# Adaptive-norm attention with a routed feed-forward: where the mask, the late weights and the keys' product stand in the attention stage

## The chip, the cores and the metric

One core of one Trainium2 chip runs the whole kernel. The metric is the time of one execution on the device in microseconds (us); of several executions the median is taken, and lower is better.

A core has a matrix engine (TensorE, PE in the profile; PEld is its weight load), a vector engine (VectorE, DVE), a scalar engine (ScalarE, ACT), GpSimd (POOL) and SyncE (SP), which here only asks for transfers. Each engine works through its own list of instructions in order, and semaphores make one engine wait for another. Transfers (DMA) asked for by SP, POOL or ACT run beside the engines.

## The reference, cut to what matters

The input `x` is 16 sequences of 512 tokens with 512 features. First comes attention with one shared head of keys and values and 16 heads of queries, 64 wide:

```python
xn  = layernorm(x) * g_in
q   = (xn @ Wq) * DH**-0.5          # 16 heads
k,v = split(xn @ Wkv)               # one head, shared; one null key and value in front
sim = q @ k.T + bias[head]          # bias: (16, 512, 512), the same for every sequence
sim = where(causal or token mask, -max, sim)
out = layernorm((softmax(sim) @ v) @ Wo) * g_out
```

Then a mixture of 16 experts follows: a root-mean-square norm, router logits, the top 512 tokens of each expert, two layers of 2048 hidden units, a weighted scatter back, and the sum with `x`.

All of the change lies in the attention. Two things matter there. The additive bias of a head is the same for all 16 sequences, and its causal part (-2^100 above the diagonal) is the same for all heads, so a bias that was once masked on the chip can be kept in device memory and read again.

## The kernel before

**Stages.** The attention stage takes the span from its start to about 1885 us; routing and the experts follow. The attention works on pairs: pair `p` is sequence `b = p // 8` and head pair `hp = p % 8`, which makes 128 pairs. `HP` is 8, `QB` (blocks of 128 queries) is 4, `DC` (chunks of 128 features) is 4, `B` is 16.

**Order.** Nearly every engine is wrapped in `Pinned` (line 119): its instructions are issued in the order in which the Python program makes them, and all of them carry line 129 in the profile. Only calls through `nc.` directly are placed by a scheduler. So the order of the loop body (`for p in range(B * HP + 1)`, from line 652) is the order on each engine. `Pair` objects overlap: while pair `p` has its scores reduced, the queries of pair `p + 1` are multiplied (`ahead`), the probabilities of pair `p - 1` are transposed and moved (`behind`), and the value product of pair `p - 2` is made (`turned.attend()`).

**The body of one pair, in order.** SP asks for the bias of pair `p + 1` (`load_bias`, tile `bias`, 1.31 MB, two buffers). PE makes the scores of blocks 3, 2 and 0 (`sp`); DVE adds the bias and takes the minimum of the negated row in one custom instruction (`reduce`: `p<-sp,bias,nn_sb`, with `nm`), ACT takes exponentials (`exps`). `late` norms get their root of mean square (`root`: a power on POOL, `rms_r`). DVE transposes the probabilities of pair `p - 1` in 32x32 squares (`behind.turn`: `sq<-p`), then 16 DMAs move the squares (`behind.move`: `pt<-sq`), ten asked for by SP and six by POOL. **Then, in the first eight pairs, POOL masks the bias of pair `p + 1`** (`mask_bias`: four affine selects of 128x256 numbers on the diagonal blocks) **and writes all of it to the device table `causal`**; from sequence 1 on `load_bias` reads `causal`. At `p == 1` POOL asks for the weights of later stages (`later_weights`, lines 195 to 200). Then come the scores and reduction of block 1, the statistics of the layer norms (`n.a()`: `ln_s`, `ln_mv`, `ln_t` on DVE and **the power on POOL**, `ln_r` or `lo_r`), the row sums, the value product `ap` with its copy `ot` on ACT, the application of the norms (`n.b()`: `xn` or `z` on DVE, for `z` also a multiplication on POOL), the division of the probabilities by their sums (`normalize`), and what `first` holds for this pair: transposes of the next sequence's normed input (`turn`: `xtp`, `xnt`), its keys and values (`keys_values`: `kp` on PE, `ka` on ACT, `vt` on DVE, and a small DMA `ka<-ka`), the transposed values (`turn_values`: `vtp`) and its token mask (`mask`: load `m8`, then `km` on DVE).

**PSUM.** `ps_s` (four buffers) holds scores, `ps_m` (three buffers) holds `qp`, `op`, `ap`, `xfp` and `kp`, `ps_t` (one buffer) holds `xtp` and `vtp`.

The order around the change in the loop body:

```python
if p + 1 < HP:
    mask_bias(p + 1, biases[p + 1])
if p == 1:
    later_weights()
...
for n in chains: n.a()
if now: now.sums()
if turned: turned.attend()
for n in chains: n.b()
...
for part in first.get(p, ()): part()     # keys_values among them
```

Of the kernel before, what the change touches and what calls it, by code (L numbers as in the profile page):

```python
# [8 lines left out]
F32 = mybir.dt.float32  # L9
# [3 lines left out]
U8 = mybir.dt.uint8  # L13
# [13 lines left out]
def tile_adaln_ffn(  # L27
# [111 lines left out]
    with ExitStack() as st:  # L139
# [54 lines left out]

        def later_weights():
            ge.dma_start(out=wo_sb, in_=wo.rearrange("(c p) n -> p c n", p=P))
            ge.dma_start(out=g_out_sb, in_=g_out.partition_broadcast(P))
            ge.dma_start(out=nw_sb, in_=norm_w.partition_broadcast(P))
            ge.dma_start(out=rw_sb, in_=router_w.rearrange("(c p) e -> p c e", p=P))
            ge.dma_start(out=rb_sb, in_=router_b.partition_broadcast(P))  # L200

# [41 lines left out]
        def load_bias(p):  # L243

            bt = biasp.tile([P, 2, SW], F32, name=f"bias_{p}", tag="bias")
            sy.dma_start(out=bt, in_=causal[p % HP] if p >= HP else bias[p])
            return bt

        def mask_bias(p, bt):


            with tc.issue_after(ge.last.ins):
                for q in range(QB):
                    diag = bt[:, :, off[q] + ext[q] - P : off[q] + ext[q]]
                    ge.affine_select(
                        out=diag, in_=diag, pattern=[[0, 2], [-1, P]],
                        compare_op=ALU.is_ge, fill=-BIG, base=0, channel_multiplier=1,
                    )
            ge.dma_start(out=causal[p], in_=bt)

        class Sequence:
# [13 lines left out]
            def turn(self, t):  # L275
# [11 lines left out]
                else:  # L287
                    ve.tensor_tensor(
                        dst, tp, g_in_sb.unsqueeze(2).to_broadcast([P, DC, P]), ALU.mult
                    )  # L290

            def mask(self):
                m8 = small.tile([DH + 1, N], U8, name=f"m8_{self.b}", tag="m8", bufs=1)
                self.km = kms[self.b % 2]
                for r in (0, DH):
                    nc.sync.dma_start(out=m8[r : r + 1, :], in_=mask[self.b : self.b + 1, :])
                for r in (0, DH):
                    ve.tensor_scalar(
                        self.km[r : r + 1, :], m8[r : r + 1, :], BIG, -BIG, ALU.mult, ALU.add
                    )  # L300

            def keys_values(self, i):

                if i == 0:
                    self.ka = seq.tile([P, N], F32, name=f"ka_{self.b}", tag="ka")
                    self.vt = seq.tile([DH, N], F32, name=f"vt_{self.b}", tag="vt")
                toks = slice(i * N // 2, (i + 1) * N // 2)  # L310
                kp = ps_m.tile([P, N // 2], F32, name=f"kp_{self.b}_{i}", tag="m")
                for c in range(DC):
                    te.matmul(
                        kp, wvk_sb[:, c, :], self.xnt[:, c, toks], start=(c == 0), stop=(c == DC - 1)
                    )
                se.activation(self.ka[DH:, toks], kp[DH:, :], AF.Identity, bias=vk_col[DH:, :])
                ve.tensor_scalar(self.vt[:, toks], kp[:DH, :], vk_col[:DH, :], None, ALU.add)
                nc.sync.dma_start(out=self.ka[:DH, toks], in_=self.ka[DH:, toks])

# [278 lines left out]

        halves, norms, routes, first, ins, loads = {}, {}, {}, {}, {}, {}
        early = HP - 3  # L600
        for b in range(B):
# [12 lines left out]
            if b + 1 <= end:  # L614
                ts, ks, v = ((0, 1, 2, 3), (2, 4), 5) if b else ((1, 2, 3, 4), (3, 5), 6)
                for t, k in enumerate(ts):
                    first.setdefault(at + k, []).append(lambda b=b, t=t: seqs[b + 1].turn(t))
                for i, k in enumerate(ks):
                    first.setdefault(at + k, []).append(lambda b=b, i=i: seqs[b + 1].keys_values(i))
                first.setdefault(at + v, []).append(lambda b=b: seqs[b + 1].turn_values())  # L620
                first.setdefault(at + 4, []).append(lambda b=b: seqs[b + 1].mask())
            if b + 2 <= end:
# [6 lines left out]
        seqs[0].xts = x0  # L629
        biases = {0: load_bias(0)}  # L630
        for pair in ((0, 1), (2, 3)):
            begun = [InNorm(seqs[0], t) for t in pair]
            for n in begun:
                n.a()
            for n in begun:
                n.b()
# [15 lines left out]
        for p in range(B * HP + 1):  # L652
            b, hp = divmod(p, HP)
            now, ahead = ahead, None
            if p + 1 < B * HP:
                biases[p + 1] = load_bias(p + 1)
                ahead = Pair(seqs[(p + 1) // HP], (p + 1) % HP)
# [18 lines left out]
            if now and behind:  # L676
                behind.turn()
                behind.move(sy, range(6, SN * SN))
                behind.move(ge, range(6))
            if p + 1 < HP:  # L680
                mask_bias(p + 1, biases[p + 1])
            if p == 1:
                later_weights()
            if 0 <= p - HP < NT // P:
# [20 lines left out]
            if now:  # L705
                now.sums()
            if turned:
                turned.attend()
            for n in chains:
                n.b()  # L710
            if now:
                now.normalize(0)
                now.normalize(3)
# [631 lines left out]
```

## Time and profile before

| what | value |
|---|---|
| median of 3 runs | 3617.39 us (3615.78 to 3621.26) |
| the profiled execution's own time | 3619.08 us |
| its span, from the first to the last instruction | 3617.40 us |
| PE busy | 3436.0 us (95%) |
| DVE busy | 2326.7 us (64%) |
| ACT busy | 1588.6 us (44%) |
| POOL busy | 904.7 us (25%) |
| `bias<-in_bias_dram` on SP, 1280 KB | 8 |
| `bias<-causal` on SP, 1280 KB | 120 |
| `causal<-bias` on POOL | 8, landing after 5.4 to 8.8 us |
| affine select on a bias, POOL | 32, median 402 ns |
| SP asks for squares (`pt<-sq`) | 1270 |
| mean granted clock of PE | 0.978 |

The profiled execution is 1.7 us above the median of the three runs, and 1.7 us longer than its span. A span counts from the first instruction to the last; busy time of one engine lies beside that of the others, and only what no other engine's work covers adds to the time. The granted clock is the share of its full clock that PE is given.

### The profile page before, as it was taken

The page shows a single profiled execution, that of the slowest core. Times are in us where ns is not written, and L with a number is a line of the kernel's source. Part 1 is how long each engine was busy: PE and PEld are TensorE (multiplying, and loading weights), DVE is VectorE, ACT ScalarE, POOL GpSimd, SP SyncE. Part 2 cuts the span into 40 slices and gives each one's busy share as a digit, 9 for nine tenths or more (in the row PEclk, how much of TensorE's full clock was granted, in tenths as well). Part 3 has the DMA queues.
Part 4 walks back from the last instruction along what each step waited for, and adds up shares of the span by engine and source line. Part 5 has one row for each costly group of instructions (what it writes and reads, how often), then busy time and mean ns, then how long its engine had stood idle before and what let it go on. Part 6 is the DMA issues. An engine that isn't in the chain of part 4 may idle for free.

```text
span 3617.4 us, 52129 instructions
## 1 busy us (share of the span) xinstructions
PE 3436.0 (95%) x16972; PEld 2477.8 (68%) x16972; DVE 2326.7 (64%) x6026; ACT 1588.6 (44%) x4160; POOL 904.7 (25%) x1332
## 2 busy tenths in 40 slices
PE   7899999999999999999993699999999999999999
PEld 3455555655556555655551588888888888888887
DVE  6676767667677777677547865555655566655553
ACT  5676667667676776667650211111112112111111
POOL 3333233333333333332320222211112112222110
PEclk9999999999999999999995899999999999999999
DMA  8877777677776666666542233333333334333330
GB/s 288 250 219 218 220 223 215 216 222 226 221 219 194 209 210 205 192 202 199 184 133 105 82 110 121 110 94 89 105 123 120 120 123 123 111 122 112 108 97 12
DMA packets 255045, 583.58 MB, mean 161 GB/s; under 512 B 48263, under 2 KB 117575, under 8 KB 236343
## 3 DMA queue, kind: packets, MB, share of 16 engines
q1 hardware_dynamic: 207360, 462.95, 38.6%
q0 software_dynamic: 45024, 114.44, 13.3%
q8 instruction: 136, 2.23, 0.3%
q10 hardware_dynamic: 2391, 2.85, 0.2%
q14 instruction: 134, 1.10, 0.1%
HBM read 366.41 MB, written 61.87 MB: 118 GB/s over the span
## 4 chain that ended last, share of the span: by engine, by line
PE 79%; DVE 8%; DMA 3%; SPq 3%; issue 2%; ACT 1%; POOL 1%; DVEq 0%; POOLq 0%; ACTq 0%
PE op L129 10%; PE r_y L129 9%; PE qp L129 9%; PE sp L129 7%; PE pa L129 6%; PE pc L129 6%; PE pc_y L129 6%; PE pa_y L129 6%; PE ap L129 6%; PE pd L129 3%; PE pe L129 3%; PE pb L129 3%; SPq L129 3%; DVE sq L129 2%; PE xfp L129 2%; DVE p L129 2%
## 5 line engine op out<-in xcount | busy, mean ns | idle before, releaser
L129 ACT ACTIVATE p<-p,nm 128x512 f32<-128x512 f32 (+3 forms) x1024 | 561.9, 550 | 256.4 <-DVE nm L129 254.9
L129 DVE CUSTOM_DVE_ANT_0 p<-sp,bias,nn_sb 128x512 f32<-128x512 f32 (+3 forms) x1024 | 499.8, 544 | 181.1 <-PE sp L129 165.4
L129 POOL DMA_DIRECT2D pt<-sq x762 | 381.3, 507 | 929.4 <-issue 561.7
L129 PE MATMUL qp<-xnt,wq_sb 128*128 128x512 f32 x1024 | 516.7, 628 | 0.0
L129 PE MATMUL op<-wo_sb,ot 128*128 128x256 f32 x1920 | 454.7, 382 | 1.1 <-ACT ot L129 1.1
L129 PEld LDWEIGHTS op<-wo_sb,ot 128*128 128x128 f32 x1920 | 358.8, 190 | 98.6 <-issue 53.9
L129 DVE STREAM_TRANSPOSE sq<-p 128x896 f32<-128x896 f32 x762 | 398.4, 587 | 25.0 <-ACT p L129 9.9
L129 ACT ACTIVATE p<-p,rs 128x512 f32<-128x512 f32 (+2 forms) x768 | 406.2, 603 | 1.8 <-DVE rs L129 1.1
L129 POOL DMA_INDIRECT out_dram<-y,tok x64 | 105.9, 1654 | 1181.0 <-ACT y L1174 1181.0
L1082 ACT ACTIVATE h<-h,b_sb 128x512 f32<-128x512 f32 (+1 forms) x256 | 143.5, 608 | 523.7 <-DVE h L129 523.7
L129 PE MATMUL sp<-ka,qa 64*128 64x512 f32 (+3 forms) x2048 | 358.6, 440 | 1.6 <-ACT qa L129 1.6
L1174 ACT ACTIVATE y<-y,gg 128x512 f32<-128x512 f32 x64 | 46.2, 722 | 646.9 <-DVE y L129 646.9
L129 PE MATMUL ap<-pt,vp 128*64 128x512 f32 (+3 forms) x2048 | 306.1, 440 | 2.7 <-ACT qa L129 1.1
L129 PEld LDWEIGHTS qp<-xnt,wq_sb 128*128 128x128 f32 x1024 | 176.2, 192 | 184.5 <-issue 169.1
L129 PEld LDWEIGHTS ap<-pt,vp 128*64 128x64 f32 x2048 | 146.3, 137 | 179.0 <-issue 142.2
L129 PE MATMUL pa<-xe,w 128*128 128x256 f32 x1024 | 243.4, 381 | 0.0
L129 PEld LDWEIGHTS sp<-ka,qa 64*128 64x128 f32 x2048 | 173.7, 189 | 89.9 <-issue 84.0
L129 PE MATMUL pa_y<-w,h 128*128 128x256 f32 x1024 | 231.5, 379 | 0.0
L129 PE MATMUL r_y<-w2t,hs 128*128 128x256 f32 x1024 | 231.5, 379 | 0.0
L129 PEld LDWEIGHTS pa<-xe,w 128*128 128x128 f32 x1024 | 195.6, 191 | 26.8
L129 PEld LDWEIGHTS r_y<-w2t,hs 128*128 128x128 f32 x1024 | 194.6, 190 | 26.4
L129 PEld LDWEIGHTS pa_y<-w,h 128*128 128x128 f32 x1024 | 193.4, 190 | 25.7
(201 smaller groups left out, 5193.9 us busy)
## 6 DMA issues: line engine op xcount, KB each, us to landing
bias<-causal SPq DMA_DIRECT2D x120, 1280.0 KB
w<-in_fc_dram SPq DMA_DIRECT2D x256, 512.0 KB
pt<-sq SPq DMA_DIRECT2D x1270, 80.0 KB
pt<-sq POOLq DMA_DIRECT2D x762, 80.0 KB, 3.1
x<-in_x_dram SPq DMA_DIRECT2D x64, 256.0 KB
out_dram<-in_x_dram SPq DMA_DIRECT2D x64, 256.0 KB
table<-xf SPq DMA_DIRECT2D x64, 256.0 KB
bias<-in_bias_dram SPq DMA_DIRECT2D x8, 1280.0 KB
```

Of the source, the lines that this page charges most:

```text
L129: self.last = tc.keep_in_program_order(made(*args, **kwargs))
L1082: nc.scalar.activation(a[0], a[1], AF.Gelu, bias=b1_sb[:, self.e, f : f + 1])
L1174: nc.scalar.activation(y, y, AF.Copy, scale=self.gg[:, g, self.e : self.e + 1])
```

## The change

Seven edits, all in the attention stage:

1. The later weights are asked for by SP and not by POOL, one transfer in each of the pairs 2 to 7, `wo` in two halves; they were asked for by POOL in pair 1, all five at once.
2. A bias is masked again in each of the first sequences until it is stored: `kept_in(hp)` is the sequence in which head pair `hp` is stored (0 for 6 and 7, 1 for 4 and 5, 2 for 2 and 3, 3 for 0 and 1). So there are 20 maskings (80 affine selects) and still 8 writes, two a sequence in sequences 0 to 3. Until its stored copy is read, a bias comes from `in_bias_dram`.
3. `mask_bias` moves from behind the squares' DMAs to behind `n.b()`, so the powers of the norms stand in front of it on POOL.
4. `keys_values` moves in front of `turned.attend()`, and `kp` is a tile of `ps_t` instead of `ps_m`.
5. The load of the token mask (`m8`) is split off, made on SP in program order, one pair ahead of its use.
6. The bias of pair 1 is asked for before the loop, behind the token mask of sequence 0.
7. The DMA of the keys (`ka<-ka`) is pinned to program order.

On PE only the eight `kp` matmuls change their place against `ap`. On DVE and ACT only `vt<-kp` and `ka<-kp` do.

```diff
-        def later_weights():
-            ge.dma_start(out=wo_sb, in_=wo.rearrange("(c p) n -> p c n", p=P))
-            ge.dma_start(out=g_out_sb, in_=g_out.partition_broadcast(P))
-            ge.dma_start(out=nw_sb, in_=norm_w.partition_broadcast(P))
-            ge.dma_start(out=rw_sb, in_=router_w.rearrange("(c p) e -> p c e", p=P))
-            ge.dma_start(out=rb_sb, in_=router_b.partition_broadcast(P))
+        later = [
+            (wo_sb[:, : HP // 2, :], wo.rearrange("(c p) n -> p c n", p=P)[:, : HP // 2, :]),
+            (wo_sb[:, HP // 2 :, :], wo.rearrange("(c p) n -> p c n", p=P)[:, HP // 2 :, :]),
+            (g_out_sb, g_out.partition_broadcast(P)),
+            (nw_sb, norm_w.partition_broadcast(P)),
+            (rw_sb, router_w.rearrange("(c p) e -> p c e", p=P)),
+            (rb_sb, router_b.partition_broadcast(P)),
+        ]
...
         def load_bias(p):
+            b, hp = divmod(p, HP)
             bt = biasp.tile([P, 2, SW], F32, name=f"bias_{p}", tag="bias")
-            sy.dma_start(out=bt, in_=causal[p % HP] if p >= HP else bias[p])
+            sy.dma_start(out=bt, in_=causal[hp] if b > kept_in(hp) else bias[hp])
             return bt
 
+        def kept_in(hp):
+            return (HP - 1 - hp) // 2
+
         def mask_bias(p, bt):
+            b, hp = divmod(p, HP)
+            if b > kept_in(hp):
+                return
             with tc.issue_after(ge.last.ins):
                 for q in range(QB):
...
-            ge.dma_start(out=causal[p], in_=bt)
+            if b == kept_in(hp):
+                ge.dma_start(out=causal[hp], in_=bt)
...
+            def load_mask(self):
+                self.m8 = small.tile([DH + 1, N], U8, name=f"m8_{self.b}", tag="m8", bufs=1)
+                for r in (0, DH):
+                    sy.dma_start(out=self.m8[r : r + 1, :], in_=mask[self.b : self.b + 1, :])
+
             def mask(self):
-                m8 = small.tile([DH + 1, N], U8, name=f"m8_{self.b}", tag="m8", bufs=1)
+                m8 = self.m8
                 self.km = kms[self.b % 2]
-                for r in (0, DH):
-                    nc.sync.dma_start(out=m8[r : r + 1, :], in_=mask[self.b : self.b + 1, :])
...
-                kp = ps_m.tile([P, N // 2], F32, name=f"kp_{self.b}_{i}", tag="m")
+                kp = ps_t.tile([P, N // 2], F32, name=f"kp_{self.b}_{i}", tag="t")
...
-                nc.sync.dma_start(out=self.ka[:DH, toks], in_=self.ka[DH:, toks])
+                sy.dma_start(out=self.ka[:DH, toks], in_=self.ka[DH:, toks])
...
-                    first.setdefault(at + k, []).append(lambda b=b, i=i: seqs[b + 1].keys_values(i))
+                    kvs.setdefault(at + k, []).append(lambda b=b, i=i: seqs[b + 1].keys_values(i))
                 first.setdefault(at + v, []).append(lambda b=b: seqs[b + 1].turn_values())
+                first.setdefault(at + 3, []).append(lambda b=b: seqs[b + 1].load_mask())
                 first.setdefault(at + 4, []).append(lambda b=b: seqs[b + 1].mask())
...
         biases = {0: load_bias(0)}
+        seqs[0].load_mask()
+        biases[1] = load_bias(1)
...
             if p + 1 < B * HP:
-                biases[p + 1] = load_bias(p + 1)
+                if p > 0:
+                    biases[p + 1] = load_bias(p + 1)
...
-            if p + 1 < HP:
-                mask_bias(p + 1, biases[p + 1])
-            if p == 1:
-                later_weights()
+            if 2 <= p < 2 + len(later):
+                sy.dma_start(out=later[p - 2][0], in_=later[p - 2][1])
...
                 now.sums()
+            for part in kvs.get(p, ()):
+                part()
             if turned:
                 turned.attend()
             for n in chains:
                 n.b()
+            if p + 1 < B * HP:
+                mask_bias(p + 1, biases[p + 1])
```

More of the change, by code (lines that the diff above doesn't have):

```diff
@@ L594, in tile_adaln_ffn @@
         end = B - 1
-        halves, norms, routes, first, ins, loads = {}, {}, {}, {}, {}, {}
+        halves, norms, routes, first, ins, loads, kvs = {}, {}, {}, {}, {}, {}, {}
         early = HP - 3
```

## The prediction

> **What bounds the kernel now.** I read the page first: engine totals and the slices.
>
> ```profile
> PE 3436.0 (95%) x16972; PEld 2477.8 (68%) x16972; DVE 2326.7 (64%) x6026; ACT 1588.6 (44%) x4160; POOL 904.7 (25%) x1332
> ...
> PE   7899999999999999999993699999999999999999
> ...
> PEclk9999999999999999999995899999999999999999
> DMA  8877777677776666666542233333333334333330
> ```
>
> PE is the bound nearly everywhere; the exceptions are the first two slices and the change of stage near 1900 us, which no edit touches. So I asked for windows. A window runs from a sequence's first bias reduction on DVE to that of the next; the rows are sequences 0, 1, and 4 to 14.
>
> ```profile
> core 0: us, PE busy (x) PEld busy (x) DVE busy (x) ACT busy (x) POOL busy (x), PEclk, DMA share, GB/s
> 24.70:142.30 117.60, 89.25 (x403) 40.30 (x401) 74.98 (x250) 71.33 (x200) 43.20 (x90) 0.88 0.85 275
> 142.30:256.20 113.90, 110.88 (x572) 65.22 (x573) 79.29 (x263) 79.71 (x222) 33.67 (x61) 0.99 0.72 221
> 488.70:1755.80 1267.10, 1246.18 (x6562) 742.26 (x6560) 888.79 (x2932) 882.62 (x2454) 396.43 (x700) 1.00 0.68 210
> ```
>
> Sequence 0 has no output projection beside it, so PE has the least to do there, and yet it is the longest: PE stands 28.4 us (117.60 - 89.25) and is granted 0.88 of its clock. Later, PE stands 3.0 us in sequence 1 and 1.9 us a sequence in the last row. Next, who ends the waits in sequence 0: on PE, then on DVE.
>
> ```profile
> PE sp L129 <- DVE nm L129: 24.8, 8, 9.2
> ...
> DVE xn L129 <- POOL ln_r L129: 22.9, 5, 6.8
> DVE p L129 <- PE sp L129: 6.5, 2, 6.0
> DVE p L129 <- POOL bias L129: 6.4, 2, 4.4
> ```
>
> PE waits for DVE, and DVE waits for POOL's power. Why a 0.6 us power is late is seen on POOL's timeline in pair 1:
>
> ```profile
> 40.10 3.03 POOL L129 DMA_DIRECT2D pt<-sq  x6 [7.28 <-DVE sq L129]
> 43.91 1.49 POOL L129 TENSOR_SCALAR_AFFINE_SELECT bias<-bias 128x256 f32<-128x256 f32 x4 [0.79 <-DMA bias<-in_bias_dram]
> 45.70 0.58 POOL L129 DMA_DIRECT2D causal<-bias  x1 [0.30 <-POOL bias L129]
> 46.28 0.92 POOL L129 DMA_DIRECT2D wo_sb<-in_wo_dram  x1
> ...
> 49.55 1.21 POOL L129 TENSOR_TENSOR ln_r<-ln_t,mhalf 128x1 f32<-128x1 f32 x2
> ```
>
> The power stands behind a mask that waits for a bias to land, behind the write and behind five weight requests. For the later sequences, the waits on PE (143 to 1756 us):
>
> ```profile
> PE kp L129 <- ACT ot L129: 18.0, 27, 1.6
> PE sp L129 <- DVE nm L129: 8.4, 22, 1.6
> ```
>
> `kp` takes a buffer of the three-buffer pool that `ap` has just used, and so waits for `ap`'s copy `ot`. These 18 us are PE time in a stage bound by PE.
>
> **The change part by part.** The sum is against the profiled execution, 3619.1 us (span 3617.4 and 1.7 around it).
>
> *Sequence 0: powers in front, weights to SP, six writes gone, bias 1 early.* DVE waits 22.9 us for powers. Pair 1 by the new order: POOL's moves end at 43.13, the two powers (1.21) at 44.34; DVE has its row sums at 43.36, so `xn` starts near 43.75 and not at 50.18, and with 1.16 + 0.9 + 0.7 of work the next reduction starts near 46.5 instead of 52.25: 5.8 us of the 6.8. The mask now follows at 44.34 and ends, with its 1.49 and 0.3 to be seen, at 46.1: just covered. Five waits with about 0.5 us left in each save 20.4. New is DVE's wait for a mask behind a power; it had 6.4 us of mask waits caused by late biases, and I leave 4 of them: 2.4 saved. Early bias 1 gives nothing by itself: pair 0's powers would start near 30.2 and end about 31.9, the mask at 33.4, and DVE starts pair 1 at 33.7 in the trace. The removed writes give room: the six that leave are 1.31 MB each, 3.9 us of all engines at the 333 GB/s of the fullest pair (estimate), 24 us of 117.6 at a DMA share of 0.85. That makes biases land sooner; it is how the 2.4 comes about and isn't counted again. Sum -22.8; I take **-22**. Bounds: nothing under 78.5 us of PE work (89.25 x 0.88) can be reached, so at most -39; if moved squares pace the pairs at 13 us, the length of its best pairs with transposes now, -12.
>
> The clock: windows of 20 us show 0.74 at 40 to 60 us, around the 9.2 us gap, and 0.83 to 0.92 up to 160 us; from 160 us it is 1.00. [...] The row is less simple: 60 to 80 us has 0.91 with no gap above 2.0. I count none of it extra: in this sequence DVE is late, and a faster PE waits longer. [...]
>
> *Weights on SP.* Six requests at about 0.5 us, 3 us of SP over six pairs. Two halves of `wo`, 1.05 MB or 3.1 us of DMA each, go past in pairs 2 and 3, behind that pair's squares and in front of the x tile and the bias of pair 4; that bias then has most of a pair (12 us) to land, and loads take 4 to 8 us by their packet times. 0; without this cover up to +3. First use is pair 9.
>
> *kp in front of ap.* 27 waits go. PE's `kp` (1.74 us of 8 x 0.215, the timeline's step) then runs before `ap` (2.37). The stall could go to three places. First, `xtp` behind `ap` in the pairs at offset 2 needs `kp` out of the single `ps_t` buffer: `ka` 0.47 and `vt` 0.48 behind `kp`, about 1.1 us with `ap`'s 2.37 as cover. If ACT or DVE is over 1.3 us late there, the wait is back. Second, `ot` comes 1.74 later on ACT and holds the divisions behind it; ACT has 1.69 us of idle time in front of the next pair's exponentials in the pair at 202 us, and the `ka` that followed (0.47) is gone from behind, so this is covered. Third, DVE waits 36.4 us for `ka` before `vt`; that idle time moves to the middle of the pair, and `xn` behind it waits for a power there anyway. The constant 0.8 us of the pairs at offset 4 go whole (14 x 0.78 = 10.9); of the 7.1 at offset 2, where ACT is late, half. **-14** (between -18 and -6).
>
> *Start.* `kp` is in the single buffer also before the loop. The second half started at about 15.4 us; now it waits for `vt` of the first, 16.98. **+1.6**. Bias 1 also shares the DMA engines with `wq` until 17 us and stands in front of `ka<-ka`; `ka` is due at 25: 0, at worst +3.
>
> *Twelve more masks, six writes moved.* A masked bias must land 1.8 us sooner (1.48 and 0.3). DVE's waits in sequences 1 to 15 show "`DVE p <- DMA bias<-causal`: 9.2, 7, 2.2": seven loads of 120 land after DVE is ready. By packet times the ones ahead of pairs 10 and 18 land 1.3 and 1.0 us before use. PE absorbs some 2 us of a late reduction where it has work, nothing in pairs that already show a gap. I take 0.6 and 0.8 for pairs 10 and 18, 1.5 for 19 and 2.2 for 26, whose loads run beside a write (8 us to land, by the row of landings); pairs 12, 17 and 25 wait for the mask behind `z`'s multiplication by under 1 us, covered. **+5** (0 to +14). The write in POOL's queue stands in front of the root `rms_r` and six squares; it issues in 0.57 us and waits for nothing but the mask.
>
> [...] The row of the 32 selects now, beside a busy DVE, is 396/402/594 ns: the longest lost 0.2. I take the row: 0; DVE is 70% busy there in any case.
>
> *Token mask a pair early.* DVE waits 13.0 us for it in four pairs (b even), where PE shows gaps of 0.9 and 1.0 at `xfp`: **-1**. Pinning `ka<-ka` leaves SP's order as it was: 0.
>
> Sum: -22 - 14 + 1.6 + 5 - 1 = -30.4, so 3588.7 for an execution like the profiled one; the median lies 1.7 under it: **3587**.
>
> **The rivals.**
>
> *The wait at `kp` only changes its place*, to `xtp` or to the divisions. For: one buffer instead of three. Against: the 2.37 us of cover. Then +14: about 3601.
>
> [...]
>
> *The moved writes collide (slower).* In sequence 0 the pairs with a write show PE gaps of 9.2, 2.0, 8.0 and 4.1 us. If the six writes in sequences 1 to 3, where projections, copies and table writes are added (DMA share 0.72; a write adds 3.9 us to pairs of 12 to 16), each cost PE 8 us, that is 48 in place of 5: 3587 - 5 + 48 = 3630. It decides from 6 us a write up. Against: their loads have 1 to 10 us in hand, and of the 9.2 us gap 6.8 are the power's queue.
>
> *It all cancels:* half of the gain in sequence 0, none at `kp`, masks at their upper end: -11 + 1.6 + 10, within noise of 3617.
>
> **How the numbers follow.** 0.2% (7.2 us) is about what a measurement of this kernel tells from no change. The sum as it stands 0.52 (3578 to 3598), `kp` moves 0.18, clock recovers 0.10, writes cost some more (3603 to 3610) 0.06, cancels 0.06, collision 0.08. So faster 0.86, same 0.06, slower 0.08. The range 3573 to 3610 leaves out the last two and the edges.
>
> **What would show it.** In the changed profile: sequence 0 near 96 us, with DVE's wait for `ln_r` under 5 us there; no `kp <- ot` line on PE, and no new `xtp <- vt` above 4 us; sequences 2 to 14 about 1 us shorter each; granted clock above 0.95 before 140 us; sequences 1 to 3 not over 3 us longer each than those after. It is wrong if PE's `sp <- nm` in sequences 1 to 3 sums to over 15 us, or if sequence 0 stays above 108 us.

## The result, and the profile after

The changed kernel takes 3592.4 us (median of 6 runs, 3585.9 to 3593.8); the kernel before, run beside it, takes 3617.2 (6 runs, 3615.8 to 3621.3). The ratio is 0.9927 [0.9915, 0.9940]. The profiled execution took 3592.75 us with a span of 3590.7: 26.7 us less span than before, where the prediction had 30.4 less.

The page of the changed kernel: engine totals, then the slices.

```profile
PE 3433.0 (96%) x16972; PEld 2473.2 (69%) x16972; DVE 2333.5 (65%) x6026; ACT 1584.9 (44%) x4160; POOL 922.0 (26%) x1375
...
PE   7899999999999999999991899999999999999999
...
PEclk9999999999999999999995899999999999999999
DMA  7877777777776666666632334333334334333330
```

PE's busy total is within 3 us of that before (3436.0), so what went is idle time. The slices are too coarse to show where. The same windows as in the prediction show it: sequences 0, 1, and 4 to 14, each from its first bias reduction to that of the next.

```profile
core 0: us, PE busy (x) PEld busy (x) DVE busy (x) ACT busy (x) POOL busy (x), PEclk, DMA share, GB/s
26.40:128.80 102.40, 85.76 (x404) 39.65 (x401) 77.73 (x251) 71.50 (x201) 39.92 (x84) 0.93 0.78 244
128.80:241.80 113.00, 110.89 (x572) 64.99 (x573) 81.78 (x262) 78.93 (x220) 43.94 (x87) 0.98 0.79 248
476.70:1733.60 1256.90, 1245.01 (x6559) 738.47 (x6557) 889.03 (x2932) 878.89 (x2454) 396.33 (x700) 1.00 0.69 212
```

With the same windows for the other sequences, and with sequence 15 counted to the first reduction of the last pair, the balance by stage is:

| stage | before | after | difference |
|---|---|---|---|
| start, to the first bias reduction | 24.7 | 26.4 | +1.7 |
| sequence 0 | 117.6 | 102.4 | -15.2 |
| sequences 1 to 3 | 346.4 | 348.0 | +1.6 |
| sequences 4 to 14 | 1267.1 | 1256.9 | -10.2 |
| sequence 15 | 112.2 | 107.9 | -4.3 |

Together that is -26.4 of the 26.7. Two traces of the changed kernel differ by up to 3 us in single sequences (sequence 1 took 113.0 and 114.5, sequence 3 took 118.1 and 115.1), so rows are read to some 2 us. Three rows are not what the sum had: sequence 0 gives 15 and not 22, sequences 4 to 14 give less than `kp` alone should, and sequence 15 gives 4.3, for which the sum had next to nothing. The experiments are about these.

The waits in sequence 0, on PE and then on DVE (us in total, times, longest):

```profile
PE sp L129 <- DVE nm L129: 10.4, 11, 3.2
PE ap L129 <- DMA nw_sb<-in_norm_w_dram: 3.5, 1, 3.5
...
DVE xn L129 <- POOL ln_r L129: 6.1, 5, 1.6
DVE p L129 <- POOL bias L129: 6.1, 5, 4.6
DVE sq L129 <- DMA nw_sb<-in_norm_w_dram: 4.8, 1, 4.8
```

The wait for the power fell from 22.9 to 6.1 us, and PE's wait behind it from 24.8 to 10.4. The waits for masks stayed near their 6.4 (6.1 now; POOL in turn waits 4.1 us for biases to land), and a wait of 4.8 us behind a transfer is new. POOL's timeline in pair 1, to be laid beside that of before:

```profile
42.04 3.02 POOL L129 DMA_DIRECT2D pt<-sq  x6 [6.58 <-DVE sq L129]
45.07 1.08 POOL L129 TENSOR_TENSOR ln_r<-ln_t,mhalf 128x1 f32<-128x1 f32 x2
46.13 1.84 POOL L129 TENSOR_SCALAR_AFFINE_SELECT bias<-bias 128x256 f32<-128x256 f32 x4
```

The powers now follow the squares at once. That is edits 1 and 3 together: neither the mask nor the weight requests stand in front of them. In sequences 1 to 14 (129 to 1733 us), PE's waits are:

```profile
PE sp L129 <- DVE nm L129: 17.6, 23, 2.6
PE xtp L129 <- DVE vt L129: 0.9, 1, 0.9
```

`kp <- ot`, 18.0 us before, is gone, and what came at `xtp` is 0.9. But `sp <- nm` rose from 8.4 to 17.6: DVE is late somewhere that it was not before.

### The profile page after: what moved, and what is told of

It is laid out like the page before. It is cut to its first block, busy times and chain, and to the rows that moved or that the text cites. A ratio compares the mean times of both kernels' runs of the same rounds, so it can differ in the third digit from the quotient of the medians.

```text
span 3590.7 us, 52220 instructions
## 1 busy us (share of the span) xinstructions
PE 3433.0 (96%) x16972; PEld 2473.2 (69%) x16972; DVE 2333.5 (65%) x6026; ACT 1584.9 (44%) x4160; POOL 922.0 (26%) x1375
## 4 chain that ended last, share of the span: by engine, by line
PE 83%; DVE 6%; DMA 2%; SPq 2%; issue 1%; POOL 1%; ACT 0%; DVEq 0%; POOLq 0%; ACTq 0%
PE op L129 11%; PE qp L129 10%; PE r_y L129 9%; PE sp L129 8%; PE ap L129 6%; PE pc L129 6%; PE pa L129 6%; PE pc_y L129 6%; PE pa_y L129 6%; PE pb L129 3%; PE pd L129 3%; PE pe L129 3%; PE xfp L129 2%; SPq L129 2%; DVE sq L129 2%
## 5 line engine op out<-in xcount | busy, mean ns | idle before, releaser
L129 PEld LDWEIGHTS r_y<-w2t,hs 128*128 128x128 f32 x1024 | 194.6, 190 | 26.4
```

What stands on the lines that cost most here:

```text
L129: self.last = tc.keep_in_program_order(made(*args, **kwargs))
```

## The experiments

Pairs are named by sequence and position here: pair 5.0 is the first pair of sequence 5. Every experiment ran beside the kernel before, whose median lay between 3617 and 3622 us, so ratios are compared and not times; sequences are compared by their windows. Edits 5, 6 and 7 have no run of their own.

**Edit 4 alone.** The kernel before with `kp` in `ps_t` and in front of `attend`.

```diff
-                kp = ps_m.tile([P, N // 2], F32, name=f"kp_{self.b}_{i}", tag="m")
+                kp = ps_t.tile([P, N // 2], F32, name=f"kp_{self.b}_{i}", tag="t")
...
+            for part in kvs.get(p, ()):
+                part()
             if turned:
                 turned.attend()
```

> The kernel before with edit 4 alone (keys' product in front of the value product, in the single buffer). Theory: the 27 waits of kp for ot (18.0 us) go and do not come back elsewhere; the pairs at offset 4 go from 16.6 to 15.7 us, the start is 1.6 us later. Together 13 to 18 us less than before: 3599 to 3604. Rival (the wait only changes its place, to xtp or to the divisions): within 5 us of before, with waits of xtp for vt above 4 us on PE.

Measured: 3603.6 us against 3620.8, ratio 0.9956 [0.9939, 0.9972]; span 3603.2, which is 14.2 less than before. PE's waits from 145 to 1741 us (sequences 1 to 14), and the window of sequences 4 to 14:

```profile
PE sp L129 <- DVE nm L129: 13.3, 26, 1.7
...
PE xtp L129 <- DVE vt L129: 0.2, 1, 0.2
...
489.70:1741.90 1252.20, 1242.41 (x6559) 737.29 (x6557) 888.60 (x2932) 877.69 (x2454) 396.35 (x700) 1.00 0.70 213
```

The 18 us went and did not move to `xtp`. Sequences 1 to 14 are 16.5 us shorter together; the best of sequences 4 to 14 fell from 114.4 to 113.0, which is also the best in the changed kernel. Part of the stall did move: `sp <- nm` rose from 8.4 to 13.3. The start grew by 2.9 us (24.7 to 27.6), and the difference is about the net 14. This part of the change is settled. It also makes the later stage stranger: with edit 4 alone, sequences 4 to 14 gain 14.9 us (1267.1 to 1252.2), and with all edits only 10.2.

**Edit 3 alone.** The kernel before, with the mask of the first eight biases behind the norm's powers.

```diff
-            if p + 1 < HP:
-                mask_bias(p + 1, biases[p + 1])
...
             for n in chains:
                 n.b()
+            if p + 1 < HP:
+                mask_bias(p + 1, biases[p + 1])
```

> The kernel before with edit 3 alone: the mask goes behind n.b(), so the powers stand in front of it; all eight biases are still stored in sequence 0, the weights are still asked for by POOL in pair 1 (still in front of that pair's powers). Theory: the order on POOL is the larger part of what sequence 0 lost, DVE's waits for ln_r there fall from 22.9 to some 10 us (pair 1 keeps most of its own), and 8 to 13 us go: 3604 to 3609. Rival (the eight writes that fill the DMA engines are the cause): under 4 us, over 3613, since the squares and biases still wait behind the writes.

Measured: 3616.1 us against 3620.8, ratio 0.9990 [0.9981, 1.0000]; sequence 0 is 113.2 us, 4.4 less. POOL's timeline in pair 1 shows what is left in front of the powers:

```profile
43.43 0.95 POOL L129 DMA_DIRECT2D wo_sb<-in_wo_dram  x1
45.83 0.56 POOL L129 DMA_DIRECT2D g_out_sb<-in_g_out_dram  x1 [1.45 <-DMA causal<-bias]
...
48.21 1.25 POOL L129 TENSOR_TENSOR ln_r<-ln_t,mhalf 128x1 f32<-128x1 f32 x2
```

Now the weight requests stand in front of the power, and one of them waits 1.45 us for a write. Moving the mask is not enough while its neighbours on the queue stay, and while all eight writes stay in sequence 0 (PE waits 6.9 us at `ap` for a transfer here). The expectation was too high.

**Edit 2 alone.** The kernel before with masks repeated and writes spread over four sequences, the masks where they were, in front of the powers.

```diff
+        def kept_in(hp):
+            return (HP - 1 - hp) // 2
...
-            if p + 1 < HP:
+            if p + 1 < B * HP:
                 mask_bias(p + 1, biases[p + 1])
```

> The kernel before with edit 2 alone: two biases stored a sequence, masks at their old place (in front of the powers), weights on POOL in pair 1. Theory of the writes: a write of 1.31 MB takes the DMA engines for some 3.5 us, in which the squares stand still, so with six of eight writes gone from sequence 0 it loses 8 to 12 us (117.6 to 106 to 110), while sequences 1 to 3 gain at most 3 us: 3606 to 3612. Rival (the order on POOL is what matters, writes do not): sequence 0 stays above 113.

Measured: 3624.1 us against 3616.8, ratio 1.0018 [1.0007, 1.0028]: slightly slower. Windows of sequences 0 to 3:

```profile
24.70:134.00 109.30, 87.50 (x402) 39.43 (x401) 74.82 (x251) 71.89 (x201) 41.71 (x89) 0.91 0.74 235
134.00:253.50 119.50, 111.23 (x572) 65.68 (x573) 78.96 (x263) 79.17 (x220) 43.66 (x87) 0.99 0.73 232
253.50:377.30 123.80, 116.68 (x600) 68.88 (x598) 81.01 (x269) 80.31 (x224) 43.90 (x83) 0.97 0.73 228
377.30:499.00 121.70, 115.55 (x600) 68.42 (x598) 81.43 (x269) 80.66 (x224) 38.31 (x69) 0.97 0.73 227
```

Sequence 0 gains 8.3 us, and sequences 1 to 3 lose 18.6 (365.0 against 346.4). From 134 to 500 us DVE waits for a power up to 6.4 us at a time:

```profile
DVE xn L129 <- POOL ln_r L129: 32.3, 12, 6.4
...
DVE z L129 <- POOL lo_r L129: 26.6, 11, 5.6
```

So edit 2 needs edit 3. Alone they give -4.4 and -8.3 in sequence 0, and edit 2 takes 18.6 back later; together, with the others, sequence 0 gives -15.2 and sequences 1 to 3 cost next to nothing. In sequence 0 that is little more than the two added up; the gain of having both is in the later sequences. No run has these two edits and no other. The slower rival of the prediction had the place right (sequences 1 to 3), but the danger was a mask in front of a power and not the write in front of a load.

**Weights back on POOL.** The changed kernel with edit 1 undone.

```diff
-            if 2 <= p < 2 + len(later):
-                sy.dma_start(out=later[p - 2][0], in_=later[p - 2][1])
+            if p == 1:
+                for out_w, in_w in later:
+                    ge.dma_start(out=out_w, in_=in_w)
```

> The changed kernel with edit 1 undone: POOL asks for the later weights in pair 1, in front of that pair's powers, in six transfers. Theory: the powers of pair 1 come 3.5 us later and the squares of pair 2 wait in POOL's queue behind the weights, so sequence 0 gets 4 to 7 us longer. Six more DMAs on POOL also bring the 2.7 us pause back to about where it was in the kernel before (last pairs of sequences 4 and 9, second of sequence 15), which gives back 8 and takes 4: 3591 to 3597 in all. Rival (weights on SP stand in front of biases and squares as they did on POOL): sequence 0 gets no longer.

Measured: 3592.1 us, ratio 0.9932 [0.9916, 0.9949], beside 0.9927 for the changed kernel: the same. The start is 2.1 us longer, and sequence 0 is 104.9 us, 2.5 longer, where 4 to 7 were expected. Sequences 1 and 2 are 2.3 and 3.0 longer and sequence 3 is 3.1 shorter. But sequences 5 and 10 take 113.0 each, where the changed kernel takes 117.5 and 117.3, and sequence 15 takes 112.0 and not 107.9. So edit 1 earns a little at the start and in sequence 0, and something that goes with it costs as much later, from two pairs far from any weight.

**What happens in pairs 5.0 and 10.0.** In the changed kernel, POOL's timeline around the end of pair 5.0, then DVE's and PE's rows behind it (in brackets the idle time before):

```profile
597.98 1.04 POOL L129 DMA_DIRECT2D pt<-sq  x2 [10.36 <-issue]
601.80 1.96 POOL L129 DMA_DIRECT2D pt<-sq  x4 [2.77 <-issue]
603.77 0.57 POOL L129 TENSOR_TENSOR lo_r<-lo_t,mhalf 128x1 f32<-128x1 f32 x1
...
604.37 0.55 DVE L129 TENSOR_SCALAR z<-z,lo_mv,lo_r 128x512 f32<-128x512 f32 x1 [4.40 <-POOL lo_r L129]
...
606.63 0.27 PE L129 MATMUL sp<-km,one_sb 64*128 64x256 bf16 x1 [2.60 <-DVE nm L129]
```

Between two of six squares' requests that need nothing from each other, POOL stands 2.77 us, and the trace names no releaser ("issue"). The power of the output norm is behind it, then `z`, then the next pair's reductions, then PE. Counting over the attention stage, such a pause stands in front of the 129th DMA that POOL asks for, and then in front of every 121st further one (250, 371, 492, 613); the number of POOL's other instructions ahead of the first and between the next ones varies (310, 185, 170). The kernel before has its pauses at the same counts, in other places (at the 613th POOL waits for a transfer anyway, and none can be told apart). The change takes seven of POOL's DMAs away ahead of the first count (five requests for weights, and two writes that come later) and five ahead of the others, so each pause falls later in the program: those of pairs 2.3, 4.7, 7.3 and 9.7 now fall in 2.4, 5.0, 7.4 and 10.0, and the one of 15.0 (in front of the 734th) leaves the position that hurts. At position 0 the power, `z` and the next reduction follow each other, and the pair itself is 2.8 us longer (14.5 against 11.7). Mostly the two pairs behind it are longer too, 29.5 us together against 27.8 with the weights on POOL. But not always: with the broadcast rows later (below), pair 5.0 is as long, and the two behind it take 27.8. So a pause there costs 2.7 to 4.5 us; at positions 4, 5 and 7 the pair is no longer than without it, at position 3 it is some 1.3 us longer. Sequences 5 and 10 are 4.5 and 4.3 us longer than with the weights on POOL. That is what sequences 4 to 14 lack; other sequences gained some, so they stand only 4.7 us behind edit 4 alone. Sequence 15 is 4.3 us shorter.

**Four more DMAs for POOL.** This is the changed kernel with four small loads ahead of the loop, into a tile that is filled later anyway.

```diff
+        for i in range(4):
+            cut = slice(4 * i, 4 * i + 4)
+            ge.dma_start(out=rb_sb[:, cut], in_=null_bias[cut].partition_broadcast(P))
```

> The changed kernel with four small extra transfers asked for by POOL before the loop (columns of the router bias tile, overwritten later). POOL shows a pause of 2.7 us between two squares' DMAs ahead of its 129th, 250th, 371st and so on DMA in both kernels: by count of DMAs. In the changed kernel it falls in the pairs at offset 0 of sequences 5 and 10, in front of the power lo_r that DVE waits for. Theory: with four more DMAs it falls into the last pairs of sequences 4 and 9, where it costs nothing; sequences 5 and 10 go from 117.4 to about 113 us, 7 to 9 us less: 3583 to 3586. Rival (the pause belongs to these pairs, or to a count of instructions): sequences 5 and 10 stay, 3591 to 3594.

Measured: 3594.2 us, ratio 0.9927 [0.9910, 0.9944]. The pauses moved by exactly four requests: out of pair 5.0 to 4.7, and sequence 5 fell from 117.5 to 113.2. There the six squares of pair 5.0 run without a break:

```profile
601.07 2.99 POOL L129 DMA_DIRECT2D pt<-sq  x6 [7.69 <-issue]
604.08 0.57 POOL L129 TENSOR_TENSOR lo_r<-lo_t,mhalf 128x1 f32<-128x1 f32 x1
```

The total gained nothing: one pause reached only the first request of pair 10.0 (sequence 10 stays at 117.7), one now stands in pair 2.3 (sequence 2 is 3.0 longer), and one is back in 15.0 (sequence 15 takes 112.2 again). The place followed the count as expected, and the count is of requests and not of bytes, since these four are small. The time did not follow, since four was the wrong number.

**Five fewer DMAs for POOL.** The changed kernel, with five small loads ahead of the loop on ACT's queue instead of POOL's.

```diff
-            nc.gpsimd.dma_start(
+            nc.scalar.dma_start(
                 out=vk_col[j * DH : (j + 1) * DH, :], ...
...
-        nc.gpsimd.dma_start(out=nb_sb, in_=null_bias.partition_broadcast(P))
+        nc.scalar.dma_start(out=nb_sb, in_=null_bias.partition_broadcast(P))
```

> The changed kernel with the five small loads before the loop (null keys, values and bias) asked for by ACT instead of POOL, in front of the query weights. Theory: the 2.7 us pause goes by count of DMAs asked for by POOL, so with five fewer it moves from offset 0 of sequences 5 and 10 to offset 1, and from offset 4 of sequences 2, 7 and 12 to offset 5; at offset 1 no power of an output norm is behind it, at offset 5 PE has more work: sequences 5 and 10 go from 117.4 to 113 to 114, the rest stays: 3583 to 3587. Rival (a pause costs the same at any pair with a power behind it): 4 us more in sequences 2, 7 and 12 or in 5 and 10: 3591 or more.

Measured: 3589.0 us, ratio 0.9930 [0.9913, 0.9946], so by the ratio no faster than the changed kernel with 0.9927. The profiled execution, which was the fastest of its four, has a span of 3584.6, the shortest of all. The pauses are in 2.5, 5.1, 7.5, 10.1 and 12.5. POOL in pairs 5.0 and 5.1:

```profile
598.84 2.99 POOL L129 DMA_DIRECT2D pt<-sq  x6 [10.35 <-issue]
601.84 0.57 POOL L129 TENSOR_TENSOR lo_r<-lo_t,mhalf 128x1 f32<-128x1 f32 x1
...
610.62 0.55 POOL L129 DMA_DIRECT2D pt<-sq  x1 [2.99 <-DMA x<-in_x_dram]
614.00 2.47 POOL L129 DMA_DIRECT2D pt<-sq  x5 [2.82 <-issue]
```

Sequences 5 and 10 take 114.5 and 114.4, 3.0 and 2.9 less, and sequence 15 keeps its 108.2. The profiled span is 6.1 us shorter, about as much as these 5.9 (sequence 1 is 3.5 longer and sequence 3 is 3.0 shorter). That the pause goes by POOL's count of DMAs, and what it costs where, is shown by the windows of these two runs; a gain of the whole kernel is not. What POOL does in the pause is open: the trace has no row there.

**The mask in front of `z`'s multiplication.** In pairs 2.0 and 3.0 (13.8 us each, against 11.7 in pair 4.0) DVE waits for a mask. Rows of the changed kernel, POOL's and then DVE's:

```profile
254.04 1.48 POOL L129 TENSOR_SCALAR_AFFINE_SELECT bias<-bias 128x256 f32<-128x256 f32 x4
...
252.48 0.47 DVE L129 TENSOR_SCALAR p<-p,rs 128x128 f32<-128x128 f32 x2
...
255.56 0.75 DVE L129 CUSTOM_DVE_ANT_0 p<-sp,bias,nn_sb 128x512 f32<-128x512 f32 x1 [2.00 <-POOL bias L129]
```

The experiment puts the mask between the power and `z`'s multiplication.

```diff
+            if p + 1 < B * HP:
+                mask_bias(p + 1, biases[p + 1])
             for n in chains:
                 n.b()
-            if p + 1 < B * HP:
-                mask_bias(p + 1, biases[p + 1])
```

> The changed kernel with the mask between n.a() and n.b(): behind the power, but in front of the multiplication of z on POOL. Theory: in sequences 2 and 3 the pair at offset 0 takes 13.8 us instead of 11.7 because the mask stands behind z's multiplication; that goes, and with it PE's waits of 2.0 us in the pair behind: 4 to 8 us less than the changed kernel, 3584 to 3588. Rival (these pairs are late because of the bias loads beside a write): no change, 3591 to 3594.

Measured: 3593.8 us, ratio 0.9927 [0.9907, 0.9948]: the same. Pair 2.0 takes 13.7 us. The wait for the mask is gone, but the rows beside it grew:

```profile
252.04 1.66 POOL L129 TENSOR_SCALAR_AFFINE_SELECT bias<-bias 128x256 f32<-128x256 f32 x4
...
252.65 2.37 DVE L129 TENSOR_SCALAR p<-p,rs 128x128 f32<-128x128 f32 x2
```

The two multiplications of DVE took 2.37 us beside the select, and 0.47 (the row of 252.48) beside `z`. Of the 2.37 us the second multiplication alone has 2.03: it started beside a select and ended 0.09 us after the multiplication of `z` that POOL runs behind the selects. The theory of this experiment falls: what the order saves in waiting, DVE's own work loses beside POOL's.

**Stores one sequence later.** In the changed kernel, pair 0.6 takes 16.8 us with 5.3 of PE standing; `sq` there waits 4.8 us for DMA. This experiment has no write in sequence 0.

```diff
-            return (HP - 1 - hp) // 2
+            return (HP - 1 - hp) // 2 + 1
```

> The changed kernel with every store one sequence later (sequences 1 to 4), so none in sequence 0; eight more maskings. Theory of the writes: the pair at offset 6 of sequence 0 (16.8 us, PE waiting 5.3) stands because a write holds the DMA engines while its squares wait; without it the pair takes 12 to 13 us and sequence 0 some 97 to 99 us instead of 102.4, while masks in sequence 4 give back 2 to 4: 3589 to 3593, by the trace a clear gain in sequence 0. Rival (the broadcast of nw named by the profile is the cause): the pair stays at 16 to 17 us.

Measured: 3593.5 us, ratio 0.9934 [0.9918, 0.9951]: the same, and pair 0.6 still takes 16.2 us. The queues' traffic from 100 to 108 us (packets, MB, share of 16 engines), first in the changed kernel, then without the write:

```profile
q1 hardware_dynamic: 482, 0.89, 46.0%
q0 software_dynamic: 145, 1.31, 45.0%
```

```profile
q1 hardware_dynamic: 700, 1.48, 69.5%
q0 software_dynamic: 27, 0.04, 1.9%
```

With the write, queue 0 takes as much of the engines (45.0%) as queue 1 (46.0%), which brings SP's squares. Without it the wait at `sq` is gone, but the bias of the next pair is late instead, and its mask with it: from 104 to 112 us the engines are still some 0.9 busy (0.89 and 0.94 in two windows of 4 us). DVE's wait, then POOL's, from 100 to 122 us without the write:

```profile
DVE p L129 <- POOL bias L129: 4.3, 1, 4.3
...
POOL bias L129 <- DMA bias<-in_bias_dram: 3.8, 1, 3.8
```

**The broadcast rows later.** The changed kernel with `g_out` and `nw` asked for in pairs 8 and 9, `rw` and `rb` in pairs 4 and 5.

```diff
-            (g_out_sb, g_out.partition_broadcast(P)),
-            (nw_sb, norm_w.partition_broadcast(P)),
             (rw_sb, router_w.rearrange("(c p) e -> p c e", p=P)),
             (rb_sb, router_b.partition_broadcast(P)),
+            None, None,
+            (g_out_sb, g_out.partition_broadcast(P)),
+            (nw_sb, norm_w.partition_broadcast(P)),
```

> The changed kernel, in which SP asks for the two 128-fold broadcast rows g_out and nw in pairs 8 and 9 (sequence 1), and for rw and rb in pairs 4 and 5; nothing else changes. In the changed kernel the pair 0_6 takes 16.8 us with 5.3 us of PE standing still, and SP takes 9.5 us to hand out its squares. Theory (these two rows, which share SP's queue with the bias of pair 7 and the squares, are what makes 0_6 late): 0_6 falls to 12.5 to 14 us, sequence 0 from 102.4 to about 99 us, and the time by 2 to 4 us against the changed kernel. Rival (the write of bias 7's predecessor and the squares alone fill the engines there): 0_6 stays above 16 us and the time is the same within 1 us. Second rival: the stall goes with the rows to pairs 1_0 and 1_1, sequence 1 gets 2 to 3 us longer, and the time is the same.

Measured: 3593.7 us against 3621.8, ratio 0.9926 [0.9913, 0.9940]; pair 0.6 takes 16.0 us with 4.3 of PE standing, and sequence 0 is 101.2. The wait is there under another name:

```profile
DVE sq L129 <- DMA ka<-ka: 4.0, 1, 4.0
```

So the two rows were not the cause; the releaser named was only the transfer that ended last. Neither the rows nor the write alone makes pair 0.6 late. Take one away, and another transfer of that pair is late by about the same. No run took both away, and which order of the transfers would help is open.

**All that looked useful together.** The changed kernel with the rows later, five small loads on ACT's queue, and `kp` of sequence 0 in the three-buffer pool; and beside it the changed kernel again.

```diff
-                kp = ps_t.tile([P, N // 2], F32, name=f"kp_{self.b}_{i}", tag="t")
+                pool, tag = (ps_t, "t") if self.b else (ps_m, "m")
+                kp = pool.tile([P, N // 2], F32, name=f"kp_{self.b}_{i}", tag=tag)
```

> The changed kernel with three edits: the rows g_out and nw in pairs 8 and 9; five small loads ahead of the loop on ACT's queue instead of POOL's (so that POOL's pause falls one pair position later, off the pairs at offset 0); kp of sequence 0 in the three-buffer pool. Theory: the parts add up: pauses -3 to -4 us (as measured when made alone), start -1.6, sequence 0 -3 if the rows are what is late there; 3583 to 3586 us. Rival (sequence 0 is paced by DVE and the squares, so that a transfer moved only moves the stall): no better than the pauses alone, 3588 to 3590.

> The changed kernel unaltered, beside the other two on the same chip, for their comparison: 3592 us, ratio 0.993 to the kernel before.

Measured: 3589.3 us (3585.7 to 3592.6), ratio 0.9907 [0.9891, 0.9922], against 3599.4 (3596.0 to 3600.1) and 0.9938 [0.9924, 0.9951] for the changed kernel on that chip. The two do not overlap, so this version is faster than the changed kernel, by 10 us here. Its ratio is the lowest of the study, though its interval overlaps that of the pauses moved alone. The traces show some 5 of the 10 us: the first reduction of the last pair starts at 1834.4 us against 1839.7. The rest isn't explained: what follows has no edit, and lasts from 1749 to 1757 us in the traces of the study. The time lies in the range of the rival and not of the sum of the parts. Of the parts, only the pauses earned what was expected (sequences 5 and 10 are 114.5 and 114.4). Putting `kp` back took the wait at the start away, but not its time. The changed kernel's rows on PE, and then the joined one's:

```profile
13.63 2.59 PE L129 MATMUL kp<-xnt,wvk_sb 128*128 128x256 f32 x8
17.29 1.99 PE L129 MATMUL kp<-xnt,wvk_sb 128*128 128x256 f32 x8 [1.07 <-DVE vt L129]
```

```profile
13.39 5.68 PE L129 MATMUL kp<-xnt,wvk_sb 128*128 128x256 f32 x16
```

Without the 1.07 us pause the sixteen products end at 19.07 and not at 19.28, because each takes longer (355 ns against 286). `kp` had 265 ns each in the kernel before. Why they take longer is open.

## Why the prediction was right or wrong

**The sign and the main waits were right.** The two main waits that the prediction named, DVE's for the power and PE's for `kp`, were those that went, and 3592.4 lies in its range; 3587 was 5 us too low. That it came so near is in part luck: sequence 0 fell 6.8 us short and sequences 4 to 14 fell 1.8 short of their terms, while sequence 15 gave 4.3 that no term had.

**Sequence 0 was mis-sized: -15.2, not -22.** The term of the powers was right in kind and 3.6 us too large: 22.9 fell to 6.1, 16.8 against 20.4 expected. What failed is the step "I leave 4 of them: 2.4 saved", with the sentence that the fewer writes make biases land sooner. Mask waits stayed at 6.1 us, and pair 0.6 got a transfer wait of 4.8 that no step had. The DMA share fell from 0.85 to 0.78 only: six writes are gone, but two still stand in pairs that are just as full (0.88 in pair 0.6 and 0.97 in 0.7; pairs 0.1 to 0.7 had 0.75 to 1.01 before). The prediction's lower bound of -12 does not follow from its own 13 us a pair: eight such pairs make 104, which is -13.6. The prediction's own mark of wrong (sequence 0 over 108 us) was not reached, nor were its marks of right (near 96, and DVE's wait for `ln_r` under 5).

**`kp`: right.** -16.5 us over sequences 1 to 14 in the run of edit 4 alone, against -14 in the sum. The cover at `xtp` held (0.2 us of wait there, 0.9 in the changed kernel). The rival in which the wait only moves is refuted. The mark "sequences 2 to 14 about 1 us shorter each" was not met by sequences 2, 3, 5 and 10, for the reasons that follow.

**Start: right in size.** +1.7 us, predicted +1.6; but it was +2.9 in the run of edit 4 alone and between +1.8 and +3.8 in the other kernels that keep `kp` in `ps_t`, and the last experiment shows that the buffer's wait is not all of it.

**Masks in sequences 1 to 3.** The sum had +5 for them, less some 3 by `kp` in these three sequences of fourteen; the row came out at +1.6. The size fits, the places do not: late loads were expected in pairs 10, 18, 19 and 26, while the cost is in pairs 1.0, 2.0 and 3.0 (1.9, 2.1 and 2.1 us). The step that failed is "wait for the mask behind `z`'s multiplication by under 1 us, covered": at the end of pairs 1.0 and 2.0 the wait is 2.0 us, and at position 0 nothing covers it. The slower rival's condition, 6 us a write, was not met: `sp <- nm` sums to 7.6 us from 129 to 477 us.

**The selects beside DVE: weighed with the wrong row.** The prediction took the durations of POOL's selects (396, 402 and 594 ns), and from them a cost of 0. That row could not show what it was asked: in the kernel before, none of the 256 multiplications `p<-p,rs` and none of the 64 `xn` ran beside a select. And a delay is to be looked for on the other engine too. In the changed kernel DVE's `p<-p,rs` on 128x128 takes 423 ns on average beside a select (21 times), 279 beside nothing (119 times) and 281 beside `z`'s multiplication (116 times); four selects beside DVE's work took 1.84 us in pair 1, and 1.49 in the kernel before. `xn` takes 705 beside a select (12 times) and 542 otherwise. Most of these delays are 0.1 to 0.2 us, less than a select lasts (0.40). But one of the 12 has 1.70 us, and lasts to 0.28 us behind the fourth select:

```profile
191.72 1.48 POOL L129 TENSOR_SCALAR_AFFINE_SELECT bias<-bias 128x256 f32<-128x256 f32 x4
191.78 1.70 DVE L129 TENSOR_SCALAR xn<-x,ln_mv,ln_r 128x512 f32<-128x512 f32 x1
```

The traces of the study have five such cases among DVE's `p<-p,rs` and `xn`: 1.70 us three times, 1.34 once, and the 2.03 of the experiment with the mask moved. What makes one case long and another short is open. Together it is about 5 us of DVE over the stage (21 x 0.144 and 12 x 0.163). The row's 0 was too little. Beside `z`'s multiplication alone `p<-p,rs` shows no delay (281); the 2.03 us case, which began beside a select, lasted through that multiplication too.

**The clock: as counted.** Windows of 20 us from 40 to 160 us show 0.83, 0.91, 1.00, 0.91, 0.91 and 1.00, where before they showed 0.74, 0.91, 0.92, 0.83, 0.91 and 0.91. PE's busy time in sequence 0 fell by 3.5 us (89.25 to 85.76), and by the prediction's estimate it would be 78.5 at the full clock. The recovery to which the prediction gave 0.10 came in part only. The mark of "above 0.95 before 140 us" was met from 80 to 100 us and lost again after. The clock is also below 1.00 in windows without a long pause: 0.91 in the prediction's window of 60 to 80 us, where no gap was above 2.0 us, and in the changed kernel 0.83 from 70 to 80 us, where PE's longest pause is 1.9 us.

**The token mask: more than expected.** DVE's wait for it, 13.0 us before, fell to 0.9. With the weights back on POOL, where no pause falls on sequences 6 and 8 and that of sequence 4 is in its last pair, as in the run of edit 4 alone, these take 114.1, 113.7 and 114.0 us, against 115.3, 115.5 and 113.9 with edit 4 alone, which still has the wait: about 3 us together, where the sum had 1. The two runs differ in other edits too, so this is an estimate.

**Not foreseen at all: POOL's pause.** Moving five requests from POOL to SP was costed at nothing, with the loads' cover as the argument. The price was on the other queue: a shift of POOL's count of DMAs, +8.8 us in sequences 5 and 10, -4.3 in 15, and some 2.5 us off where it stood in pairs 2.3 and 7.3 (14.5 and 14.4 us against 13.1), so about +2 in all. The pauses were in the trace of before, as idle time of POOL with "issue" as its end.

## What to carry to other kernels

When an operation is put in front on a queue, look at everything that still stands between its inputs and it: moving the mask alone gave little, spreading the writes alone lost time, and the gain came with both, with the power first. When the DMA engines are nearly full, as in pair 0.6 (a share of 0.88), taking one transfer away can make another late: `sq` waited 4.8 us there, without the write the mask came 4.3 us late, and with the rows later `sq` waited 4.0. The named releaser is the last one and need not be the cause. And weigh what one engine's work costs another beside it by the rows of both engines, not only by those of the one that is being added to: POOL's selects showed a median of 0.40 us before and after, while DVE's `p<-p,rs` takes 423 ns beside one and 279 alone.

## What the runs showed of the hardware

- POOL stands for 2.6 to 2.9 us between two requests in front of its 129th DMA and every 121st one after that, up to the 734th in the attention stage, with 310, 185 and 170 other instructions ahead of and between the first three. (Where it waits there for something else, the pause cannot be told apart.) In the two runs that shifted the count by four and by five, the pauses moved by as many requests. On the path at position 0 one costs 2.7 to 4.5 us.
- DVE's multiplication of 128x128 by a column takes 423 ns beside an affine select and 279 alone. In five cases in all traces such a multiplication, or the norm's `xn`, that began beside a select lasted 1.3 to 2.0 us, four of them until 0.1 to 0.3 us after the last of POOL's instructions in that row.
- Two executions of the same kernel can differ by some microseconds in a stage that no edit touches (what follows attention took 1749.2 us in one trace of the changed kernel and 1754.3 in the other), and by up to 3 us in a single sequence. So a change of a few us in the total says little, and one in a single sequence is sure only where another trace shows it again.
